# Issuing A of the first block behind x on one queue, with eleven zero matmuls fewer around B's product

## The chip, the cores and the metric

The kernel runs on one core of a Trainium2 chip. The metric is the device time of one execution in microseconds (us), as the median of several runs. A profiled execution gives, beside its time, a trace of every instruction and DMA packet; its span runs from the first to the last instruction of the program.

## The reference

The input `x` holds 8 batches of 256 tokens with 1024 features. Each batch is first sent through a low-rank adapter of rank 16, chosen by the batch's id (3 to 7, out of eight adapters), then through a gated feed-forward layer with an inner width of 2752, and the result is added to `x`:

```python
Bx  = einsum("bni,bri->bnr", x, B[ids])         # B's product, rank 16
c   = einsum("bnr,bor->bno", Bx, A[ids])        # A's product
q   = lambda v, s: clip(v / s, -448, 448).astype(float8_e4m3fn) * s
gate = q(c, gate_in_scale) @ (gate_w * gate_w_scale).T
up   = q(c, up_in_scale)   @ (up_w * up_w_scale).T
h    = silu(gate) * up
out  = x + q(h, down_in_scale) @ (down_w * down_w_scale).T
```

The weights `gate_w`, `up_w` and `down_w` come as float32 numbers that are already fp8 values.

## The kernel before

The 2048 tokens are cut into four blocks of 512 (two batches each), numbered `t` = 0 to 3; activations lie with features on the 128 partitions and tokens along the free dimension. `x` of a block is kept in SBUF as `xs[t]`, eight slices of 128 features (`k` = 0 to 7). The inner width is cut into 22 chunks `c` of 128 rows; each chunk's gate and up weights are one tile `w_gu` of 1 MB, of which five buffers exist. The first five chunks are loaded at the very start (`load_gate_up`, line 391), chunk 0 in two halves.

The program opens with the loads. On SyncE's queue (`nc.sync`) and ScalarE's (`nc.scalar`), written out by hand in this order:

- `x` of block 0 comes in four pieces of 2, 3, 2 and 1 slices (`PIECES`, `load_x`, line 381), all on SyncE: the first two at once, the last two after B.
- `adapter_of` (line 363) reads a batch's adapter number from the small tile `ids_i` into a register of the engine that will issue the DMA.
- `load_b` (line 366) loads B of one batch, 68 KB: batch 0 on ScalarE, batch 1 on SyncE.
- `load_a_two` (line 373) loads A of one batch as two DMAs of 32 KB (16 partitions of 2048 bytes each): batch 0 on ScalarE, between the third and the fourth piece of x in the program; batch 1 on SyncE, behind the fourth piece. Both batches go into the tile `a_two[0]`.
- Then come the weights of chunks 0 to 4, and behind them B, x and A of the other blocks.

Each DMA signals its end through one of eight semaphores, taken in turn over both queues; before it is issued, its engine waits for the DMA that used the same semaphore last, that is, the eighth before it in the program.

TensorE's instructions are kept in program order (`multiply`, line 471, so most TensorE rows of the profile have this line and are told apart by their tiles). It begins with matmuls of a tile of zeros into a PSUM tile `warm` that nobody reads (`pass_time`). Then `two_times_b(0)` multiplies the two batches of block 0 by their B: for every slice `k` four matmuls of 128 tokens, each in a strip of 32 columns of the array, into two PSUM tiles `bx`. `times_b` may call a function `between` after a slice; here it issues more zero matmuls after slice 6, ahead of slice 7, the one that the last piece of x brings. Four copies (line 517, two on VectorE and two on ScalarE) bring `bx` to the SBUF tile `bm`. `two_times_a(0, bm)` multiplies by A in strips of 32 rows into PSUM tiles `c`; VectorE and ScalarE round these to fp8 (`round_to`, lines 527 and 529) into `xg[0]`. Then `gate_up(0, 0)` runs the 16 matmuls of chunk 0 for block 0 (`y`, eight slices for gate and eight for up), and `gate_up(1, 0)` and so on follow with chunks 1 to 4. Block 1's adapter, block 1's chunks 0 to 4, then blocks 2 and 3 come next; from chunk 5 on every chunk is used for all four blocks. The down product with its additions and stores is the last third.

The call around the change is:

```python
        warm = psum.tile([P, TB], F32, tag="ps", name="warm")
        pass_time(warm, 16, TB)
        bm = two_times_b(0, lambda k: pass_time(warm, 4) if k == 6 else None)
        pass_time(warm, 7)
        two_times_a(0, bm)
        gate_up(0, 0, turns=(2, 2, 2, 2))
```

Of the kernel before, what the change touches and what calls it, by code (L numbers as in the profile page):

```python
# [18 lines left out]
P = 128  # L19
# [9 lines left out]
TB = 512  # L29
# [254 lines left out]
def adaln_ffn(  # L284
# [13 lines left out]
    nc = tc.nc  # L298
# [9 lines left out]
    zeros = const.tile([P, TB], BF16, name="zeros")  # L308
# [28 lines left out]
    with ExitStack() as fast:  # L337
# [14 lines left out]
        b_two = [lora.tile([P, 2 * BROW + R], F32, name=f"b{t}") for t in range(2)]  # L352
# [9 lines left out]
        def adapter_of(batch, queue):  # L362
            return queue.value_load(ids_i[0:1, batch : batch + 1], min_val=0, max_val=7)  # L363
# [3 lines left out]
                out=b[:, i * BROW : (i + 1) * BROW], in_=b8[bass.ds(adapter * P, P), :]  # L367
            )

        def load_a_two(t, j, adapter, queue=nc.sync):  # L370
            for g in range(2):
                row = 32 * (2 * g + j) + R * j
                queue.dma_start(  # L373
                    out=a_two[t][row : row + R],
                    in_=a8[bass.ds(adapter * 2 * R + g * R, R), :],
                )

        def load_x(t, k):
            piece, first = x_of(x4, t, k)
            ks = slice(first, first + piece.shape[1])  # L380
            nc.sync.dma_start(out=xs[t][:, ks, :], in_=piece)
# [16 lines left out]
        first, second = adapter_of(0, nc.scalar), adapter_of(1, nc.sync)  # L398
        load_b(b_two[0], 0, first, nc.scalar)
        load_b(b_two[0], 1, second, nc.sync)  # L400
        load_x(0, 5)
        load_a_two(0, 0, first, nc.scalar)
        load_x(0, 7)
        load_a_two(0, 1, second, nc.sync)
        for c in range(NFIRST):
            load_gate_up(c, parts=1 if c else 2)
        adapters = [adapter_of(2 + q, nc.sync) for q in range(6)]
# [4 lines left out]
        for j in range(2):  # L412
            load_a_two(1, j, adapters.pop(0))
# [56 lines left out]
        def multiply(*args, **kwargs):  # L470
            tc.keep_in_program_order(nc.tensor.matmul(*args, **kwargs))  # L471

        def pass_time(to, n, size=P):

            for i in range(n):
                multiply(
                    to[:, :size],
                    lhsT=zeros[:, :P],
                    rhs=zeros[:, :size],
                    start=(i == 0),  # L480
                    stop=(i == n - 1),
                )

        def times_b(bx, b, n, quads, between=None):


            for k in range(NH):
                for q, (i, row, t, cols) in enumerate(quads):
                    at = i * BROW + k * R - row
                    multiply(  # L490
                        bx[q][32 * q : 32 * (q + 1)],
                        lhsT=b[:, at : at + 32],
                        rhs=xs[t][:, k, cols],
                        start=(k == 0),
                        stop=(k == NH - 1),
                    )
                if between:
                    between(k)

        def two_times_b(t, between=None):  # L500


            n = SEQ // 2
            quads = [
                (j, R * j, t, slice(at, at + n))
                for half in range(2)
                for j in range(2)
                for at in (j * SEQ + half * n,)
            ]
            bx = [psum.tile([P, n], F32, tag="ps", name=f"bx{half}") for half in range(2)]  # L510
            times_b([bx[q // 2] for q in range(4)], b_two[t], n, quads, between)
            bm = lora.tile([P, 2, n], F32, tag="bm2", name="bm2", bufs=2)
            for other in range(2):
                for half, copy in enumerate((nc.vector.tensor_copy, nc.scalar.copy)):
                    to = half ^ other
                    tc.keep_in_program_order(
                        copy(  # L517
                            bm[64 * to : 64 * (to + 1), other],
                            bx[half][64 * half : 64 * (half + 1)],
                        )  # L520
                    )
            return bm
# [8 lines left out]
        def two_times_a(t, bm):  # L531


            n = SEQ // 2
            for part in range(2):
                cs = [psum.tile([P, 2, SEQ], F32, tag="ps", name=f"c{q}") for q in range(4)]
                for other, i in product(range(2), range(2)):
                    for q in range(4):
                        rows = slice(32 * q, 32 * (q + 1))
                        multiply(  # L540
                            cs[q][:, i, bass.ts(q // 2 ^ other, n)],
                            lhsT=a_two[t][rows, bass.ts(2 * part + i, P)],
                            rhs=bm[rows, other],
                            start=True,
                            stop=True,
                        )
                for q in range(4):
                    k = KS * part + 2 * (q // 2)
                    to = xg[t][:, k : k + 2, bass.ts(q % 2, SEQ)]
                    round_to(to, cs[q], nc.vector if q % 2 else nc.scalar)  # L550

        def four_times_b():
            quads = [(q, 0, 2 + q // 2, bass.ts(q % 2, SEQ)) for q in range(4)]
            bx = psum.tile([P, SEQ], F32, tag="ps", name="bx")
            times_b([bx] * 4, b_four, SEQ, quads)
            bm = lora.tile([P, SEQ], F32, tag="bm", name="bm", bufs=2)
            nc.vector.tensor_copy(bm, bx)
            return bm
# [73 lines left out]


        warm = psum.tile([P, TB], F32, tag="ps", name="warm")
        pass_time(warm, 16, TB)
        bm = two_times_b(0, lambda k: pass_time(warm, 4) if k == 6 else None)
        pass_time(warm, 7)
        two_times_a(0, bm)
        gate_up(0, 0, turns=(2, 2, 2, 2))
        for c in range(1, NFIRST - 1):  # L640
            gate_up(c, 0)
        bms = []
        gate_up(NFIRST - 1, 0, between=(12, lambda: bms.append(two_times_b(1))))
        two_times_a(1, bms[0])
        gate_up(0, 1, turns=(2, 2, 2, 2))
# [85 lines left out]
        for k in range(NH - 1):  # L731
# [23 lines left out]
            first = k % 2 == 0  # L755
# [29 lines left out]
    with found_others.Else():  # L785

        k = NH - 1
# [9 lines left out]
        t, cols = NTB - 1, slice(cut, TB)  # L797
# [88 lines left out]
```

## Time and profile before

| what | value |
|---|---|
| median of 3 runs | 475.93 us (475.82 to 476.24) |
| the profiled execution's own time | 475.75 us |
| its span | 474.0 us |
| TensorE matmuls busy | 469.6 us, 2514 of them |
| ScalarE busy | 192.5 us |
| VectorE busy | 105.6 us |
| mean DMA busy share, 0 to 40 us | near full from 3 us on |
| zero matmuls (`warm`) | 27, 6.6 us busy |
| first `bx` matmul of block 0 | 6.77 us |
| first `c` matmul of block 0 | 9.98 us |
| first `y` matmul of block 0 | 12.12 us |

Times in the table's last three rows are counted from the span's start. Busy time of TensorE includes overlap of pipelined matmuls, so the distance between the starts of two matmuls says more on its pace than the length of one. A line of the timeline gives start, length, engine, line, operation, tiles written and read, shape and count, and in square brackets the idle time before it and what ended that. "PEld" is the load of the stationary operand, which runs beside the matmuls. "SPq" is SyncE's queue, "ACTq" ScalarE's.

### The profile page before, as it was taken

What the parts mean: (1) busy time and instruction counts of PE and PEld (TensorE: products, weight loads), DVE (VectorE), ACT (ScalarE), POOL (GpSimd) and SP (SyncE); (2) the same over time, 40 slices, a digit from 0 to 9 for tenths busy, and PEclk for the clock granted to TensorE, in tenths of its full rate; (3) what the DMA queues carried; (4) which work ended last, traced back from release to release, by engine and by line L of the source; (5) the groups of instructions that cost most, each with busy time, mean ns of one, the idle gap of its engine ahead of it and who ended that gap; (6) DMA issues with size and microseconds to landing.
All of it is one profiled execution on the core that took longest, in us unless ns stands there. A gap on an engine that the chain in (4) does not pass through costs nothing.

```text
span 474.0 us, 6007 instructions
## 1 busy us (share of the span) xinstructions
PE 469.6 (99%) x2514; PEld 217.1 (46%) x2514; DVE 105.6 (22%) x163; ACT 192.5 (41%) x249; POOL 1.0 (0%) x7
## 2 busy tenths in 40 slices
PE   8999999999999999999999999999999999999997
PEld 5454544444444444444444444444444444444444
DVE  2332521212212121222212121232120121031031
ACT  2332438995555745443354544359212022021000
POOL 0000000000000000000000000000000000000000
DMA  8995023322222112222210121133335255163031
GB/s 316 416 406 153 1 90 115 153 89 90 89 89 90 54 45 80 90 89 89 90 57 36 41 62 56 61 100 106 115 135 162 66 184 160 28 212 110 3 116 67
DMA packets 13781, 53.45 MB, mean 113 GB/s; under 512 B 1650, under 2 KB 2930, under 8 KB 10802
## 3 DMA queue, kind: packets, MB, share of 16 engines
q1 hardware_dynamic: 13536, 52.86, 31.8%
q8 instruction: 21, 0.34, 0.3%
q10 hardware_dynamic: 210, 0.14, 0.1%
q14 instruction: 14, 0.11, 0.1%
HBM read 44.60 MB, written 8.39 MB: 112 GB/s over the span
## 4 chain that ended last, share of the span: by engine, by line
PE 96%; DMA 2%; ACTq 0%; ACT 0%; issue 0%; DVE 0%
PE y L471 62%; PE yd L471 32%; DMA w_gu<-w_gu 1%; PE c L471 1%; PE bx L471 1%; DMA a<-a 1%; ACT L307 0%; ACTq L373 0%; ACTq L306 0%; ACTq L366 0%; DVE o L696 0%; ACTq L363 0%; PE count L471 0%
## 5 line engine op out<-in xcount | busy, mean ns | idle before, releaser
L471 PE MATMUL y<-xg,w_gu 128*128 128x512 fp8e4 x1376 | 298.2, 379 | 0.1
L471 PEld LDWEIGHTS <-w_gu 128*128 128x128 bf16 x1376 | 134.1, 98 | 162.8 <-issue 1.3
L471 PE MATMUL yd<-hid,w_d 128*128 128x512 fp8e4 (+2 forms) x693 | 146.0, 373 | 0.0
L610 ACT ACTIVATE g<-y,gate_s 128x512 f32<-128x512 f32 (+1 forms) x88 | 59.8, 681 | 136.3 <-PE y L471 136.3
L611 DVE SCALAR_TENSOR_TENSOR hid<-y,up_by_down,g 128x512 fp8e4<-128x512 f32 x84 | 63.1, 751 | 219.4 <-PE y L471 161.6
L471 PEld LDWEIGHTS <-w_d 128*128 128x128 bf16 x693 | 66.6, 98 | 79.0 <-issue 1.7
L457 ACT ACTIVATE junk<-w_d 128x1408 bf16<-128x1408 uint16 (+1 forms) x16 | 21.2, 1324 | 88.5 <-DMA w_d<-w_d 88.4
L696 DVE SCALAR_TENSOR_TENSOR o<-yd,down_s,x 128x512 f32<-128x512 f32 x28 | 20.0, 748 | 107.3 <-PE yd L471 92.5
L457 ACT ACTIVATE junk<-w_gu 128x2048 bf16<-128x2048 uint16 (+1 forms) x22 | 41.0, 1863 | 0.0
L464 ACT ACTIVATE junk<-hid 128x2048 bf16<-128x2048 fp8e4 x21 | 40.0, 1904 | 0.4
L464 ACT ACTIVATE junk<-xg 128x2048 bf16<-128x2048 fp8e4 x8 | 15.3, 1909 | 0.3
L529 ACT ACTIVATE xg<-c,inv 128x512 fp8e4<-128x512 f32 x16 | 9.7, 688 | 8.6 <-PE c L471 8.6
L527 DVE TENSOR_SCALAR xg<-c,inv 128x512 fp8e4<-128x512 f32 x16 | 10.9, 745 | 2.8 <-PE c L471 2.8
L471 PE MATMUL warm<-zeros 128*128 128x512 bf16 (+1 forms) x27 | 6.6, 404 | 1.2 <-DVE zeros L309 1.2
L696 DVE SCALAR_TENSOR_TENSOR o<-yd,down_s,xg 128x512 f32<-128x512 f32 (+2 forms) x5 | 3.2, 644 | 12.3 <-PE yd L471 12.3
L517 ACT COPY bm<-bx 64x128 f32<-64x128 f32 x4 | 1.0, 262 | 9.2 <-PE bx L471 9.2
L471 PEld LDWEIGHTS <-zeros 128*128 128x128 bf16 x27 | 2.6, 117 | 4.8 <-issue 3.1
L471 PE MATMUL bx<-x,b 128*32 128x128 f32 x128 | 4.3, 276 | 0.1
L471 PE MATMUL c<-bm,a 32*128 32x128 f32 x128 | 4.3, 277 | 0.0
L457 ACT ACTIVATION_READ_ACCUMULATOR junk<-w_gu 128x1 f32 x22 | 4.2, 191 | 0.0
L471 PEld LDWEIGHTS c<-bm,a 32*128 32x128 f32 x128 | 3.9, 186 | 0.5 <-ACT bm L517 0.4
L471 PE MATMUL yd<-hid_tail,w_dt 64*128 64x512 bf16 (+1 forms) x32 | 4.1, 377 | 0.0
(47 smaller groups left out, 41.0 us busy)
## 6 DMA issues: line engine op xcount, KB each, us to landing
w_gu<-w_gu SPq DMA_DIRECT2D x20, 1024.0 KB, 4.8
outT<-o SPq DMA_DIRECT2D x31, 256.0 KB, 2.2
w_d<-w_d SPq DMA_DIRECT2D x8, 704.0 KB, 4.9
w_d<-w_d SPq DMA_DIRECT2D x8, 640.0 KB, 3.9
x<-x SPq DMA_DIRECT2D x2, 2048.0 KB, 11.3
x<-x SPq DMA_DIRECT2D x1, 1792.0 KB, 13.1
w_gu<-w_gu SPq DMA_DIRECT2D x3, 512.0 KB, 4.2
x<-x SPq DMA_DIRECT2D x2, 512.0 KB, 3.9
```

Of the source, the lines that this page charges most:

```text
L457: nc.scalar.activation(junk_like(w), low(w), AF.Copy, accum_out=lows[:rows, column : column + 1])
L464: nc.scalar.activation(junk_like(q), q, AF.Square, accum_out=squares[:rows, column : column + 1])
L471: tc.keep_in_program_order(nc.tensor.matmul(*args, **kwargs))
L517: copy(bm[64 * to : 64 * (to + 1), other], bx[half][64 * half : 64 * (half + 1)],)
L527: nc.vector.tensor_scalar(to, c, scale, None, ALU.mult, saturate=False)
L529: nc.scalar.activation(to, c, AF.Copy, scale=scale, saturate=False)
L610: nc.scalar.activation(g[rows], gates, AF.Silu, scale=gate_s[: gates.shape[0]])
L611: nc.vector.scalar_tensor_tensor(to, in0=ups, scalar=up_by_down[rows], in1=g[rows], op0=ALU.mult, op1=ALU.mult, saturate=False,)
L696: nc.vector.scalar_tensor_tensor(o, in0=y, scalar=down_s, in1=x, op0=ALU.mult, op1=ALU.add)
```

## The change

A of batch 0 is no longer issued on ScalarE's queue. All four A pieces of block 0 are issued on SyncE's queue, behind the last piece of x, batch 1's before batch 0's; for batch 0's pieces SyncE reads the adapter number of batch 0 into a register of its own. `load_a_two` loses its `queue` argument. ScalarE still issues the ids and B of batch 0.

Of the zero matmuls ahead of B's product 15 are left of 16, all 512 columns wide. The four of 128 columns between slices 6 and 7 go, with the `between` argument that carried them. After B's product there is one of 512 columns where there were seven of 128. Twenty-seven become sixteen.

```diff
--- before.py
+++ after.py
@@ -367,10 +367,10 @@
                 out=b[:, i * BROW : (i + 1) * BROW], in_=b8[bass.ds(adapter * P, P), :]
             )
 
-        def load_a_two(t, j, adapter, queue=nc.sync):
+        def load_a_two(t, j, adapter):
             for g in range(2):
                 row = 32 * (2 * g + j) + R * j
-                queue.dma_start(
+                nc.sync.dma_start(
                     out=a_two[t][row : row + R],
                     in_=a8[bass.ds(adapter * 2 * R + g * R, R), :],
                 )
@@ -399,9 +399,9 @@
         load_b(b_two[0], 0, first, nc.scalar)
         load_b(b_two[0], 1, second, nc.sync)
         load_x(0, 5)
-        load_a_two(0, 0, first, nc.scalar)
         load_x(0, 7)
-        load_a_two(0, 1, second, nc.sync)
+        load_a_two(0, 1, second)
+        load_a_two(0, 0, adapter_of(0, nc.sync))
         for c in range(NFIRST):
             load_gate_up(c, parts=1 if c else 2)
         adapters = [adapter_of(2 + q, nc.sync) for q in range(6)]
@@ -470,18 +470,12 @@
         def multiply(*args, **kwargs):
             tc.keep_in_program_order(nc.tensor.matmul(*args, **kwargs))
 
-        def pass_time(to, n, size=P):
+        def pass_time(to, n):
 
             for i in range(n):
-                multiply(
-                    to[:, :size],
-                    lhsT=zeros[:, :P],
-                    rhs=zeros[:, :size],
-                    start=(i == 0),
-                    stop=(i == n - 1),
-                )
-
-        def times_b(bx, b, n, quads, between=None):
+                multiply(to, lhsT=zeros[:, :P], rhs=zeros, start=(i == 0), stop=(i == n - 1))
+
+        def times_b(bx, b, n, quads):
 
 
             for k in range(NH):
@@ -494,10 +488,8 @@
                         start=(k == 0),
                         stop=(k == NH - 1),
                     )
-                if between:
-                    between(k)
-
-        def two_times_b(t, between=None):
+
+        def two_times_b(t):
 
 
             n = SEQ // 2
@@ -508,7 +500,7 @@
                 for at in (j * SEQ + half * n,)
             ]
             bx = [psum.tile([P, n], F32, tag="ps", name=f"bx{half}") for half in range(2)]
-            times_b([bx[q // 2] for q in range(4)], b_two[t], n, quads, between)
+            times_b([bx[q // 2] for q in range(4)], b_two[t], n, quads)
             bm = lora.tile([P, 2, n], F32, tag="bm2", name="bm2", bufs=2)
             for other in range(2):
                 for half, copy in enumerate((nc.vector.tensor_copy, nc.scalar.copy)):
@@ -632,9 +624,9 @@
 
 
         warm = psum.tile([P, TB], F32, tag="ps", name="warm")
-        pass_time(warm, 16, TB)
-        bm = two_times_b(0, lambda k: pass_time(warm, 4) if k == 6 else None)
-        pass_time(warm, 7)
+        pass_time(warm, 15)
+        bm = two_times_b(0)
+        pass_time(warm, 1)
         two_times_a(0, bm)
         gate_up(0, 0, turns=(2, 2, 2, 2))
         for c in range(1, NFIRST - 1):
```

## The prediction

> **What bounds the kernel now.** I read the shares of the span first: TensorE (PE) has work for 469.6 of 474.0 us, so only its idle time and its pace can change the end.
>
> ```profile
> PE 469.6 (99%) x2514; PEld 217.1 (46%) x2514; DVE 105.6 (22%) x163; ACT 192.5 (41%) x249; POOL 1.0 (0%) x7
> ```
>
> Every touched instruction lies in the first 13 us, so next comes PE's part of the timeline there (start, length, instruction, count). "warm" are the zero matmuls, "bx" is B's product, "c" is A's, "y" is gate and up.
>
> ```profile
> 1.20 5.64 PE L471 MATMUL warm<-zeros 128*128 128x512 bf16 x16 [1.20 <-DVE zeros L309]
> 6.77 1.91 PE L471 MATMUL bx<-x,b 128*32 128x128 f32 x56
> 8.61 0.40 PE L471 MATMUL warm<-zeros 128*128 128x128 bf16 x4
> 9.13 0.42 PE L471 MATMUL bx<-x,b 128*32 128x128 f32 x8
> 9.49 0.56 PE L471 MATMUL warm<-zeros 128*128 128x128 bf16 x7
> 9.98 2.17 PE L471 MATMUL c<-bm,a 32*128 32x128 f32 x64
> 12.12 5.18 PE L471 MATMUL y<-xg,w_gu 128*128 128x512 fp8e4 x22
> ```
>
> The same timeline of the weight loads (PEld) shows what PE waits for: 0.23 us and 0.30 us for x, and after the 16 matmuls of chunk 0 it waits for chunk 1's weights:
>
> ```profile
> 8.03 0.38 PEld L471 LDWEIGHTS bx<-x,b 128*32 128x32 f32 x16 [0.23 <-DMA x<-x]
> 9.13 0.16 PEld L471 LDWEIGHTS bx<-x,b 128*32 128x32 f32 x8 [0.30 <-DMA x<-x]
> 15.82 0.12 PEld L471 LDWEIGHTS <-w_gu 128*128 128x128 bf16 x2 [0.59 <-DMA w_gu<-w_gu]
> ```
>
> The 0.59 is the load's idle time, not PE's loss: in the trace's records y matmuls start 216 ns apart, and this once 477 ns (15.35 to 15.83). PE loses **0.26 us** there. The chain of waits, cut to 0 to 40 us, puts the same transfer on the path:
>
> ```profile
> 8.78 7.00 DMA w_gu<-w_gu
> 15.78 0.05 issue
> 15.83 13.12 PE y L471 x60
> ```
>
> From 15.83 to 470.9 us no two matmul starts lie more than 0.32 us apart: TensorE never waits for data again. So the whole forecast is one question: when does chunk 1 of gate and up start, now 15.83 us? Everything after it follows at a fixed distance.
>
> Two things gate that start. (a) Chunk 1's landing at 15.78. (b) TensorE's own chain: last x piece, bx, the bm copies, c, xg, chunk 0; alone it would reach chunk 1 at 15.35 + 0.22 = 15.57, so it has 0.26 us to spare.
>
> Why does (a) land so late? The DMA view says that the engines are full (mean share 1.00 or more from 3 us on in the table by stretches). Of chunk 1's sixteen shares fifteen land at 14.11 to 14.30 and one at 15.78 (landing events of its semaphore); the earlier transfers have no such straggler. In between, one engine moves a packet of another kind, which the DMA view of 13.5 to 14.6 us shows:
>
> ```profile
> q8 instruction: 1, 0.02, 5.9%
> ```
>
> It is a 16 KB packet of 1.03 us at 13.56. That share stays 1.3 to 1.5 us behind for chunks 2 to 4 too (18.11 against 16.79 for chunk 2), without harm, since TensorE needs chunk 2 only at 19.3.
>
> [...] the first zero matmuls start 427 ns apart, those from 5.38 us on 216 ns, 4.2 us after the first. [...]
>
> **The change, part by part.**
>
> *One zero matmul fewer at the start* (16 to 15): 216 ns. The last one starts at 6.46, B's second piece has landed at 6.44, so bx can start about 0.2 us earlier, near 6.55. It then runs into the x wait at 8.03, so it is worth 0 (hidden by x).
>
> *Four small ones fewer between the parts of bx, seven small ones after bx turned into one wide one.* Their starts are 56 ns apart. Both groups sit in waits (x's last piece until 9.13; the bm copies, DVE from 9.59, until c at 9.98), so as time they cost 0 now and return 0. What they did is keep the array busy: the wait before the last bx matmuls becomes an idle stretch of about 0.5 us, that before c one of about 0.3 us.
>
> *A's two DMAs for batch 0 leave ScalarE.* ScalarE has nothing until its bm copy at 9.65, so nothing there moves. The two pieces (64 KB, at about 400 GB/s 0.16 us) no longer run ahead of x's last piece: x lands about 0.16 us earlier, 8.93 instead of 9.09.
>
> *SyncE's queue gets them, with one register load of the adapter's number.* Prices from its rows: 0.57 us for a load (six take 10.58 to 13.99 with their address work), 0.2 + 0.35 us for an A DMA. Each DMA takes one of eight completion semaphores in turn and waits for the DMA eight before it; in the instruction listing all four A pieces keep places 6 to 10 in that count, and every weight DMA keeps its own. Now SyncE stands 0.9 us before its last A piece until x's second piece lands (5.97), which the waits of its queue show:
>
> ```profile
> SPq L391 <- DMA a<-a: 1.6, 2, 1.2
> SPq L373 <- DMA x<-x: 0.9, 1, 0.9
> ```
>
> After the change: x's last piece leaves at 3.84 as now; A of batch 1 at 4.56 and 5.13; register load to 6.05; A of batch 0 at 6.3 and 6.85. The 0.9 us wait is used up by that work. The first weight DMA goes at 7.2 instead of 6.36, the second at 7.65 instead of 7.20. Chunk 1's goes *earlier*: it waited until 8.78 for ScalarE's second A piece (the 1.2 us above) and now waits for an x piece that has landed at 7.99, so about 8.1. Chunk 2's waits for x's last piece, 9.0 instead of 9.15.
>
> Does the later first weight DMA leave the DMA engines dry? x's last piece and A occupy them until 8.1 to 8.5 (packet records). The first x DMA needed 1.03 us from issue to first packet; 7.2 + 1.03 = 8.23. So the gap is 0 to 0.15 us; its upper bound, if the whole 0.84 us delay less the 0.3 us of backlog came through, is 0.5 us. I take 0. The lower bound is 0 as well, as the bytes are the same.
>
> A itself now lands behind x: its last piece was last in line before too (9.46) and stays there. c needs it at about 9.8: 0.35 us to spare.
>
> Sum: chain (b) gets 0.16 us earlier (15.41); landing (a) stays at 15.78, because the bytes ahead of it and the fetch are the same. Chunk 1 starts at 15.83: **change 0**. The profiled execution took 475.75 us (span 474.0 and 1.75 around it), the median of three is 475.93, 0.18 above; the forecast is 475.9.
>
> **Rivals.**
>
> *The straggler moves away (gain).* If the instruction fetch at 13.56 follows TensorE's position in its program, 22 instructions fewer put it up to 11 y matmuls, 2.4 us, later. Chunk 1 then lands at 14.3, and (b) decides: 0.26 + 0.16 = 0.42 us less, 475.5. Against it: the first five such packets come at 13.56, 24.83, 36.28, 48.50 and 60.85 us, 11.3 to 12.4 us apart whether PE ran 51 or 162 matmuls between them; only later do they come every 128 matmuls. More than 0.42 us is not to be had.
>
> *The DMA engines run dry* for 0.1 to 0.5 us ahead of the weights: chunk 1 lands later by that much, 476.0 to 476.4.
>
> *TensorE's clock falls back (slower).* [...] If c's stretch is the slow one: 64 matmuls of 1.9 us and bx's last eight doubled, 2.0 - 0.42 = +1.6, 477.5. It decides as soon as (b) loses over 0.42 us. For it: these fillers sit exactly in the two x waits and the bm wait. [...]
>
> *That the change does not do what it says* can be left out: the instruction listing has 16 zero matmuls for 27, and all four A DMAs on SyncE behind x.
>
> **How the numbers follow.** Forecast as summed: 0.44. Straggler moves: 0.15. Dry DMA: 0.12, mostly within 0.2%. Clock falls: 0.26. Something unseen: 0.03. The bound of 0.2% is 0.95 us, about what a measurement of this kernel can tell from no change. Within it lie the first three, 0.67 after a small tail; slower is 0.30; faster needs 0.95 us where only 0.42 is in sight, 0.03. The likeliest case alone spans 475.7 to 476.2. The range must take in the clock's case to leave out no more than 2 in 10: 475.4 (0.42 less, and 0.1 of spread) to 477.5.
>
> **What would show it.** Right: y's start near 12.0, chunk 1's load again with a wait on w_gu at 15.8, y starts 216 ns apart from the first, first weight DMA at 7.2 and chunk 1's at 8.1 on SyncE. The clock rival: y or c matmuls 427 ns or twice as far apart between 8.8 and 15.6, and no wait for w_gu. The straggler rival: no wait before chunk 1 and a landing near 14.3. Wrong altogether: any gap in TensorE after 16 us that was not there.

## The result, and the profile after

The changed kernel takes 478.48 us (median of 5, 478.14 to 478.73), the kernel before 475.85 us beside it: ratio 1.0054 (95% interval 1.004 to 1.0069), 2.63 us slower. The profiled executions differ by 2.8 us of span (476.8 against 474.0). The forecast was 475.9, with a range up to 477.5.

TensorE's part of the timeline over the first 26 us of the changed kernel:

```profile
1.19 6.08 PE L471 MATMUL warm<-zeros 128*128 128x512 bf16 x15 [1.19 <-DVE zeros L309]
7.20 1.97 PE L471 MATMUL bx<-x,b 128*32 128x128 f32 x64
9.11 0.39 PE L471 MATMUL warm<-zeros 128*128 128x512 bf16 x1
9.59 2.18 PE L471 MATMUL c<-bm,a 32*128 32x128 f32 x64
11.71 3.63 PE L471 MATMUL y<-xg,w_gu 128*128 128x512 fp8e4 x16
16.31 9.89 PE L471 MATMUL y<-xg,w_gu 128*128 128x512 fp8e4 x45 [0.98 <-DMA w_gu<-w_gu]
```

Chunk 0 starts at 11.71, earlier than before by 0.41 us: the last piece of x landed at 8.70 instead of 9.09 us, and B's product no longer splits. Chunk 1 starts at 16.31 instead of 15.83, because its weights land at 16.27. The sixteen y start 216 ns apart, and the granted clock is 1.00 in every stretch from 6 to 16 us: it has not fallen. So far 0.49 us are lost.

The same view of 28 to 41 us holds the next loss. These lines are of the changed kernel:

```profile
29.37 1.96 PE L471 MATMUL bx<-x,b 128*32 128x128 f32 x64
31.26 1.04 PE L471 MATMUL y<-xg,w_gu 128*128 128x512 fp8e4 x4
32.22 2.05 PE L471 MATMUL c<-bm,a 32*128 32x128 f32 x59
35.27 0.49 PE L471 MATMUL c<-bm,a 32*128 32x128 f32 x5 [1.00 <-issue]
35.70 5.57 PE L471 MATMUL y<-xg,w_gu 128*128 128x512 fp8e4 x25
```

and these of the kernel before:

```profile
31.74 2.14 PE L471 MATMUL c<-bm,a 32*128 32x128 f32 x64
33.81 7.51 PE L471 MATMUL y<-xg,w_gu 128*128 128x512 fp8e4 x34
```

Block 1's 64 c matmuls run through before; now TensorE stops for 1.00 us with five left, and "issue" in the brackets says that it waited for nothing that the profile shows: no semaphore, no transfer of data. (Its brackets count from the modelled end of the last matmul; from start to start the stop is 1.28 us.) The chains of waits of the two kernels, the changed one first, give the start of the y behind the c:

```profile
35.77 4.42 PE y L471 x20
```
```profile
33.87 6.15 PE y L471 x28
```

That is 1.90 us later, of which 0.49 is old: 1.41 us lost here.

The third loss lies at the only branch that TensorE executes, in the view of 440 to 460 us; first the changed kernel, then the one before:

```profile
453.59 0.61 PE L471 MATMUL yd<-hid_tail,w_dt 64*128 64x512 bf16 x4
454.93 0.60 PE L471 MATMUL yd<-hid_tail,w_dt 64*128 64x512 bf16 x4 [0.74 <-issue]
455.47 4.71 PE L471 MATMUL yd<-hid,w_d 128*128 128x512 fp8e4 x21
```
```profile
451.69 1.03 PE L471 MATMUL yd<-hid_tail,w_dt 64*128 64x512 bf16 x8
452.66 5.57 PE L471 MATMUL yd<-hid,w_d 128*128 128x512 fp8e4 x25
```

Here yd is the down product and hid_tail the last 64 rows of the inner width. Four of the eight hid_tail matmuls stand ahead of the branch and four in its Else part. What follows them begins at 455.47 instead of 452.66: 2.81 us later, 0.91 more than the 1.90. The instructions of the branch's own line show why (count, then the shortest, median and longest duration in ns, and the first and last start); first the changed kernel, then the one before:

```profile
L772 PEldq COMPARE_BRANCH  x1: 3788/3788/3788, 451.1 to 451.1; - x1
```
```profile
L780 PEldq COMPARE_BRANCH  x1: 481/481/481, 449.2 to 449.2; - x1
```

TensorE's sequencer (PEldq) takes 3.79 us for the branch instead of 0.48. It begins the branch 2.5 us before the first of the four hid_tail matmuls that stand ahead of it starts (451.08 against 453.59 us; 449.19 against 451.69 before), so most of the 3.79 us passes while TensorE still works on what stands ahead of the branch: the fourth of these matmuls starts at 453.82, and the next one at 454.93, just after the branch ends at 454.87. Both kernels carry a prefetch hint for this branch, executed 10.1 us ahead of it (at 440.97 and 439.07 us), and still the branch took 3.79 us in the changed kernel. The sum is 0.49 + 1.41 + 0.91 = 2.81 us, the whole difference in span. None of it is where the removed matmuls stood.

### The profile page after: what moved, and what is told of

It is laid out like the page before. It is cut to its first block, busy times and chain, and to the rows that moved or that the text cites. A ratio compares the mean times of both kernels' runs of the same rounds, so it can differ in the third digit from the quotient of the medians.

```text
span 476.8 us, 5987 instructions
## 1 busy us (share of the span) xinstructions
PE 469.9 (99%) x2503; PEld 216.8 (45%) x2503; DVE 105.6 (22%) x163; ACT 192.6 (40%) x249; POOL 1.0 (0%) x7
## 4 chain that ended last, share of the span: by engine, by line
PE 96%; DMA 2%; SPq 1%; issue 1%; DVE 0%
PE y L471 62%; PE yd L471 31%; DMA w_gu<-w_gu 2%; PE c L471 1%; PE bx L471 1%; SPq L373 0%; DMA ids_i<-ids 0%; SPq L363 0%; SPq L381 0%; SPq L391 0%; SPq L366 0%; DVE o L688 0%; PE count L471 0%
## 5 line engine op out<-in xcount | busy, mean ns | idle before, releaser
L471 PE MATMUL warm<-zeros 128*128 128x512 bf16 x16 | 6.5, 580 | 1.2 <-DVE zeros L309 1.2
L471 PE MATMUL c<-bm,a_four 16*128 16x256 f32 x64 | 4.1, 389 | 0.0
```

## The experiments

**Three theories.** F: both stalls come from where TensorE's instructions lie within blocks of 16 KB. That is the size of each of the 21 packets of queue q8, whose kind the profile names "instruction" (0.34 MB in both kernels); that TensorE stops when such a block is late is what the theory supposes. The kernel lost eleven zero matmuls, each a weight load and a matmul (2514 of each before, 2503 after), 22 instructions; everything behind has moved up by 22 places. Q: the moved A transfers hold up the weights and the instruction packets. C: the zeros mattered as work that keeps the array busy.

**1. Only A moved.**

```diff
-        load_a_two(0, 0, first, nc.scalar)
         load_x(0, 7)
-        load_a_two(0, 1, second, nc.sync)
+        load_a_two(0, 1, second)
+        load_a_two(0, 0, adapter_of(0, nc.sync))
```

> The kernel before with only A of batch 0 moved to SyncE's queue; all 27 zero matmuls stay, so TensorE's program is that of before. Theory F (where TensorE's instruction blocks end): the stalls inside block 1's c (1.4 us) and at the branch (0.9 us) come from the 22 TensorE instructions that are missing, so both are absent here; only chunk 1's later landing is left, 0.5 us, so 476.3 us. Theory Q (the queue): the moved transfers delay weights and instruction fetches, all 2.6 us stay, 478.5 us.

Measured: 476.32 us, ratio 1.001 (1.0003 to 1.0017). In its TensorE timeline c runs through, and chunk 1 waits for its weights:

```profile
16.07 1.69 PE L471 MATMUL y<-xg,w_gu 128*128 128x512 fp8e4 x7 [0.69 <-DMA w_gu<-w_gu]
31.99 2.14 PE L471 MATMUL c<-bm,a 32*128 32x128 f32 x64
```

By the medians moving A is 0.47 us of the loss. It makes no stall (the branch takes 486 ns), so Q falls as the cause of the stalls. In the traced execution chunk 1 starts 0.24 us later than before and the time is 0.23 us longer (475.98 against 475.75), so the late landing is all that is lost there; how late it is differs among the traces (experiments 9 and 10).

**2. Only the zero matmuls changed.**

```diff
-        pass_time(warm, 16, TB)
-        bm = two_times_b(0, lambda k: pass_time(warm, 4) if k == 6 else None)
-        pass_time(warm, 7)
+        pass_time(warm, 15, TB)
+        bm = two_times_b(0)
+        pass_time(warm, 1, TB)
```

> The kernel before with only the zero matmuls changed to 15 and 1; A of batch 0 stays on ScalarE's queue. Theory F: both stalls are there, 1.4 + 0.9 us, and chunk 1 lands as before, so 478.1 us. Theory Q: nothing but the loss of fillers, 475.9 us.

Measured: 477.67 us, ratio 1.0036 (1.0026 to 1.0047). Both stalls are there, at the same matmuls: again five c are left, and four hid_tail matmuls stand ahead of the second gap (the branch takes 3.77 us):

```profile
31.43 2.05 PE L471 MATMUL c<-bm,a 32*128 32x128 f32 x59
34.55 0.49 PE L471 MATMUL c<-bm,a 32*128 32x128 f32 x5 [1.07 <-issue]
```
```profile
454.19 0.60 PE L471 MATMUL yd<-hid_tail,w_dt 64*128 64x512 bf16 x4 [0.72 <-issue]
```

The two halves of the change, 0.47 and 1.82 us, make 2.29 of the 2.63 us. That this run is under the 478.1 expected of F fits its trace: chunk 1 starts at 15.53 us without a wait, 0.30 earlier than before.

**3. The length given back without the work.** To the changed kernel:

```diff
+        pass_time(warm, 11, 1)   # size=1: one column each
         pass_time(warm, 15)
```

> The changed kernel with eleven zero matmuls of one column each ahead of the fifteen: TensorE's program is as long as before, at a cost of well under 1 us in a stretch that waits for x, and the array does almost no more work. Theory F: both stalls go, 476.3 us. Theory C (the zeros mattered as work that keeps the array busy): one-column matmuls bring nothing back, 478.5 us, with the two stalls still there.

Measured: 476.23 us, ratio 1.001 (1.0002 to 1.0019). The eleven start 27 ns apart, 0.3 us in all, and both stalls are gone (the branch takes 486 ns):

```profile
32.25 2.14 PE L471 MATMUL c<-bm,a 32*128 32x128 f32 x64
```

C falls: as work they are nothing.

**4. The length given back between the two stalls.** To the changed kernel:

```diff
         two_times_a(1, bms[0])
+        idle = psum.tile([P, TB], F32, tag="ps", name="idle")
+        pass_time(idle, 11, 1)
```

> The changed kernel with eleven one-column zero matmuls behind block 1's c instead, ahead of block 1's chunk 0. Theory F: up to block 1's c the program is the shortened one, so that stall (1.4 us) stays; from there on positions are as before, so the branch stall (0.9 us) goes: about 477.6 us. If the two stalls hang together, or hang on what happens at the start, both stay (478.5 us) or both go.

Measured: 477.66 us, ratio 1.0037 (1.0024 to 1.0049). The stall that lies ahead of the eleven stays, the one behind them goes:

```profile
34.72 0.49 PE L471 MATMUL c<-bm,a 32*128 32x128 f32 x5 [0.77 <-issue]
35.14 0.43 PE L471 MATMUL idle<-zeros 128*128 128x1 bf16 x11
```
```profile
L780 PEldq COMPARE_BRANCH  x1: 486/486/486, 450.8 to 450.8; - x1
```

So each stall hangs on the number of TensorE instructions ahead of it, wherever these stand.

**5 and 6. Part of the length.** As in 3, with `pass_time(warm, 5, 1)` and `pass_time(warm, 8, 1)`.

> The changed kernel with five one-column zero matmuls at the start, 10 of the 22 missing TensorE instructions. If a stall depends on which side of an instruction-block end a piece of work lies, each stall is there whole or not at all: 476.3, 477.2, 477.7 or 478.5 us. If it grows with the number of missing instructions, both are about half as long, 477.3 us.

> The same with eight, 16 of the 22 missing instructions. Whole or not at all, as for five; at least as few stalls as with five. If stalls grow with the number missing: about a quarter, 476.8 us.

Measured, one time each: 477.21 and 476.24 us. With 12 instructions missing the c stall is there and the branch takes 486 ns; with 6 missing neither stall is there. The stall with 12 missing leaves ten c instead of five, and the next one starts 980 ns after the last:

```profile
32.20 1.84 PE L471 MATMUL c<-bm,a 32*128 32x128 f32 x54
34.75 0.60 PE L471 MATMUL c<-bm,a 32*128 32x128 f32 x10 [0.71 <-issue]
```

Five pairs more at the start move the stop five pairs forward: it keeps its place as counted in instructions, not its place in the work. Each stall is there or not: c's threshold lies between 6 and 12 missing instructions, the branch's between 12 and 22. The time for five matches the wrong entry of the list, 477.2 (branch alone) where 477.7 was written for c alone; the trace decides that it is c.

**7 and 8. One block more.** In the kernel before, from 60.85 to 445.56 us, 120 to 137 matmuls start between one 16 KB packet and the next, mostly 128, which are 256 instructions with their weight loads. If blocks of 256 instructions are the cause, 256 more must bring both stalls back, and 278 more must not. In the changed kernel, with 154 for the second:

```diff
-        pass_time(warm, 15)
+        pass_time(warm, 143, 64)
```

> The changed kernel with 143 zero matmuls of 64 columns at the start instead of 15 of 512: 256 TensorE instructions more, one block of 16 KB, in about the same 6 us, so what follows lies at the same places within its blocks as in the changed kernel. Theory F with a period of one block: both stalls are there, about 478.3 us. If instead the length itself mattered (the longer the program, the earlier the requests), no stall, 476.2 us.

> The same with 154 zero matmuls of 64 columns: 278 more than the changed kernel, so places within the blocks as in the kernel before. Theory F: no stall in c and a short branch, 476.2 us (chunk 1 still lands late). If only the number of wide zeros mattered, as for e9: the two would agree.

Measured: 478.8 us, ratio 1.0067 (1.0025 to 1.011), against 476.6 us, ratio 1.0019 (1.0011 to 1.0026). The first, with 256 more, stops at the very same c, and its branch takes 3.84 us; the second runs through with a branch of 481 ns:

```profile
31.80 2.05 PE L471 MATMUL c<-bm,a 32*128 32x128 f32 x59
35.55 0.49 PE L471 MATMUL c<-bm,a 32*128 32x128 f32 x5 [1.71 <-issue]
```
```profile
32.46 2.14 PE L471 MATMUL c<-bm,a 32*128 32x128 f32 x64
```

Eleven zero matmuls more take both stalls away again, and the medians differ by 2.2 us. That fits a period of 256 instructions; a shorter period that divides 256 would pass as well, and the 128 matmuls from packet to packet speak for 256. (The second is 0.4 us above the 476.23 of the third experiment; its block 0 c also waits 1.14 us for A, which was not followed further.)

**What all twelve traces say of the 16 KB packets.** The stop among the c lies behind the same weight load, the 348th of TensorE's program, in the changed kernel and in experiments 2, 4 and 5, and behind the 476th, 128 further on, in experiment 7. In these five traces the second 16 KB packet (the third in experiments 7 and 8, whose programs are one block longer) starts at 32.1 to 33.0 us; in the seven traces without the stop it starts at 24.8 to 26.1. In the three traces with the branch stall (the changed kernel, 2 and 7) a packet starts 1.0 to 1.1 us after the branch does; in the other nine one has started 2.5 to 3.8 us ahead of it. In all eight stalls TensorE goes on, or the branch ends, 1.25 to 1.53 us after the packet's end. So each stall goes with a packet that came late. Which instructions a packet holds no trace shows; that TensorE stood waiting for those in the late one is read from these times and counts.

**9 and 10. Why chunk 1 lands late.** Two theories: L, the first weight DMA leaves too late (7.06 us against 6.36); B, the first three weight DMAs, now 0.5 us apart (7.06, 7.52, 8.00), slow each other. In the packet records from 7 to 16 us, 22 of the 4 KB packets, the size of chunk 0's, take over 0.3 us in the changed kernel and 3 before, so something slows them. To the kernel of experiment 1, and then to the kernel before:

```diff
             load_gate_up(c, parts=1 if c else 2)
+            if c == 0:
+                adapter_of(0, nc.sync)      # read and not used
```
```diff
         load_a_two(0, 1, second, nc.sync)
+        adapter_of(0, nc.sync)              # read and not used
```

> A of batch 0 on SyncE's queue with all 27 zero matmuls (476.3 us), and one register load that nobody uses between the DMAs of chunk 0 and chunk 1 on SyncE, so that chunk 1's leaves near 8.6 us instead of 8.0, as late as before the change. Theory L (the first weight DMA leaves too late): nothing better, chunk 1 lands at 16.0 or later, 476.3 us. Theory B (three weight DMAs issued back to back slow each other's packets): slow packets go, chunk 1 lands near 15.8, 475.9 us.

> The kernel before with one register load that nobody uses on SyncE ahead of the weights, so that the first weight DMA leaves at 6.9 instead of 6.36 us, A untouched and chunk 1's DMA still at 8.8. Theory L: chunk 1 lands 0.2 to 0.5 us later, 476.2 us. Theory B: lands as before, 475.9 us.

Measured: 476.63 us, ratio 1.0016 (1.0009 to 1.0023), and 476.26 us, ratio 1.0006 (0.9997 to 1.0015). With the gap chunk 1's DMA leaves at 8.59, and its weights land later still, at 16.54; 17 packets are slow. B does not hold. With A untouched and the first weight DMA at 7.14, 9 packets are slow and chunk 1 starts at 16.07 instead of 15.83:

```profile
16.07 1.84 PEld L472 LDWEIGHTS <-w_gu 128*128 128x128 bf16 x10 [0.55 <-DMA w_gu<-w_gu]
```

That is L's direction and as much as in the trace of experiment 1, half of the 0.49 in the changed kernel's. But the interval of its time holds no change, and its traced execution loses as much again at a later wait of bx for ScalarE, so its time does not price L. The last share of chunk 1 also moves by itself: it landed at 14.77 in experiment 2 with the loads as before (15.78 in the kernel before), and at 15.79 to 16.54 in the nine traces with A moved. L is the better of the two and is not shown.

## Why the prediction was wrong

**The step that failed** is "Everything after it follows at a fixed distance", drawn from the fact that TensorE never waits after 15.83 us. That described the trace of one program, at one position of its instructions. 2.3 of the 2.8 us lie behind that point, at two stops that go with a late instruction packet (1.41 and 0.91 us). The prediction's own sign of being wrong altogether, a gap in TensorE after 16 us that was not there, is what came.

**"As time they cost 0 now and return 0"**, on the small zeros, and the 216 ns hidden by x: right as time, and experiment 3 shows it from the other side. (In the changed kernel's trace bx began at 7.20 and not near 6.55, since the zeros ran 427 ns apart for longer, up to 6.29 us, and still chunk 0 came earlier.) But the entry for each edit lacked a term: the 22 instructions as length of the program. The number stood in the text, in the rival of the straggler, and was used only for what an instruction packet does to a neighbour's data, not for a stop of TensorE at a late one.

**The regular spacing of the first five instruction packets**, taken as a sign that position does not set them, misled. In the changed kernel the second comes at 32.87 us (24.83 before), just ahead of the stall, and experiments 2 to 8 show that position does set the stalls. The branch goes with such a packet too: one lies inside its 3.79 us (452.16 to 453.43), 0.91 of which is exposed. In the stretches of y, where TensorE takes 2 instructions in 216 ns, no packet brought a stop in the two kernels: from chunk 1's start (15.83 us before, 16.31 after) no two starts there lie more than 0.32 us apart. Among block 1's c, 64 matmuls in 2 us, TensorE stopped in five of the twelve traces.

**"I take 0"** for the later first weight DMA: mis-sized. Chunk 1 started 0.49 us later in the trace, about the upper bound of 0.5 (0.47 by the medians of experiment 1, 0.24 in its trace). The issue times were right (7.06, 7.52 and 8.00 for 7.2, 7.65 and 8.1); that the later issue is the reason for the delay is not shown.

**Chain (b)** had 0.16 us to gain and gained 0.41 by chunk 0's start, as x landed 0.39 us earlier; it lay behind the landing as forecast, so it bought nothing. The wait on w_gu before chunk 1 came too, 0.49 us later than forecast. (The DMA share, read as 1.00 or more from 3 us on, is 0.98 from 16 to 18 us in the same table; nothing hangs on it.)

**The slower rival, a falling clock,** had the sign and not the cause: y starts 216 ns apart after c, and the changed kernel's mean granted clock is 1.000. That the clock would fall without the small zeros was not shown: in the trace of before, too, y starts 216 ns apart. Its chance of 0.26 carried the 0.30 for slower; its price of 1.6 us (477.5) set a range that ended 1 us short.

## What to carry to other kernels

Where instructions are removed or added on an engine that is never idle, count them as program length, and look at every dense stretch and branch behind, however far: here 22 TensorE instructions fewer before 10 us brought a stop of 1.41 us at 34 us and one of 0.91 us at 454 us. Cheap fillers of one column (eleven took 0.3 us in experiment 3) restore or shift the length without work, so they tell such a stall from a wait for data. A stop that keeps its count of weight loads from the program's start when fillers are added, as in experiment 5 (behind the 348th), is one of the program's length, and "issue" in the brackets of a timeline line, with no semaphore behind it, is the sign to try them. A trace in which an engine never waits says nothing on how close to waiting it is: that of the kernel before showed no two matmul starts more than 0.32 us apart from 15.83 us on.

## What the runs showed that was not expected

The prediction put the late last share of chunk 1 (15.78 us, the others by 14.30) down to the instruction packet of 1.03 us at 13.56. That is not shown, and experiment 2 speaks against it as the whole reason: there a packet of 1.02 us comes at 13.54, the loads are as before, and the last share lands at 14.77, 0.38 after the one ahead of it.

In one execution TensorE's clock fell after a gap of 1.71 us. In the profiled execution with 256 instructions more, the stop of 1.71 us among the c was followed, from 36.87 us on, by eight y starts 417 to 427 ns apart, and by 216 ns again after that; the granted clock in the trace is 0.50 from 36.84 to 40.25 us. In the 3.41 us ahead of that TensorE was busy for 1.70 us. That execution took 480.58 us, the other two of the kernel 478.19 and 478.8. After the gaps of 0.71 to 1.07 us in the other kernels y kept its 216 ns. What makes the clock fall is not shown: it is one execution.

Open remains what sets the moment at which an instruction packet comes: 22 instructions fewer moved the second one by 8 us, from 24.83 to 32.87, and the first hardly (13.56 and 13.73). Open is also what fills the time between a packet's end and TensorE's going on (33.94 to 35.27 us in the changed kernel).
